# Cross-attention block on one core: reciprocals one slot later, sums behind copies and loads, a product stream spread over eight slots

## The chip, the cores and the metric

The kernel runs on one core of one Trainium2 chip. The metric is the device time of one execution in microseconds. Before the change three runs took 780.96, 783.5 and 778.15 us, a median of 780.96 us. The profile is of one further execution.

## The reference

Eight sequences of 256 tokens with 512 features attend to a context of the same shape, with 16 heads of 32 features, and an MLP of width 2048 follows. All is float32.

```
x   = layer_norm(hidden, ln1);  q = x @ q_w + q_b          # heads: 16 x 32
k   = enc @ k_w + k_b;          v = enc @ v_w + v_b
p   = softmax(where(mask, q @ k.T / sqrt(32), -max))
h   = (p @ v) @ cproj_w + cproj_b + hidden
y   = gelu(layer_norm(h, ln2) @ fc_w + fc_b) @ proj_w + proj_b
out = h + y
```

## The kernel before

The eight sequences are worked in four groups of two (512 tokens). A feature dimension lies on the partitions, in chunks of 128, for everything that is multiplied.

Every large product is a 2 by 2 block product with seven block multiplications instead of eight (`strassen`, L320 to L383): the pieces p0 to p6 each put four matmuls of 128x128 by 128x256 on PE (the trace shows two instructions for each) into one of two PSUM banks and empty the bank with ACT or DVE. Such a product needs sums of the quarters of both operands, made on DVE with `sum_up` (L164 to L167): s2, s3, s4 and a sum in place of 21 for the first operand (`A_SUMS`), t1, t2, t4 and a sum in place of 12 for the other (`B_SUMS`). xnT is the normalised and transposed x; kw, qw, vw, cw are the four weights of the attention; fcw and pw those of the MLP. Only the first product, k of group 0, is made with all eight terms (`eight`, L422), so that it needs no sums.

The attention runs over 32 units: unit n is a group, four heads (a quarter of the features) and one of the two sequences. For a unit, `scores` fills four PSUM banks, one for each head; `softmax(n, j)` takes the maximum of head j on DVE (L536) and the exponential on ACT (L546), which also gives the row sums; `divide` makes the reciprocals of the sums on DVE (L558) and scales the probabilities with four instructions on POOL (L560); `turn_probs` transposes head j on PE (L571) into one of two PSUM banks, emptied by DVE for head 0 (L574) and by ACT for the others (L576); `attend` multiplies with v (L587) and copies the result with the bias of v on DVE (L595).

The order on each engine is the order in which the code is written out; there is no scheduler. The loop near the end of the attention part has one slot for each unit. Slot n issues the scores and the softmax of unit n+2, and between them the transposes and the product of unit n. Into a slot of group g with number u (0 to 7) other work is hung by two tables: `between[g, u, 0..1]` holds the pieces of the block products of the next group and the transposes that feed them, `aside[g, u, 0..3]` holds loads, sums, layer norm parts (`norm_over`: statistics, then the inverse root on POOL at L193 and L194, then the normalisation on DVE at L197), bias additions on POOL (L483) and mask work. In the loop, `aside 0` stands ahead of the first transposes, `between 0` after head 1, `aside 1` after head 3, `between 1` after the last part of the softmax, `aside 2` ahead of `attend`, and `aside 3` at the slot's end. Below, slot n counts from 0 to 31; slot 8g+u belongs to (g, u).

Units 0 and 1 are prepared in a prologue, together with the projections of group 0. The projections of group g+1 are hung into group g; the last group has none to make, and takes the output projections (`project_out`, po) of groups 1 and 2 instead, and the first layer norm, transposes and weight sums of the MLP. The residual goes through POOL additions (L494) and is stored to DRAM by `store_hid`.

`cols` holds all bias and layer norm vectors as columns; they are loaded as 44 rows by the POOL queue, transposed on PE and copied by DVE.

The MLP runs over the four groups. In each, four steps q make two chunks of the hidden layer in both halves: seven block multiplications with fcw (L865, called pf), with DVE copies at L920, L922, L924, L932 and L937 and the GELU on ACT (L908), then differences on POOL (L940, L941). The second matrix follows (py). The sums of the quarters of proj_w, each 128x2048, are made in group 0 by `sum_pw` (L874), after the loads of pw have been issued by the SP queue.

Of the kernel before, what the change touches and what calls it, by code (L numbers as in the profile page):

```python
# [22 lines left out]
def tile_xattn_block(  # L23
# [45 lines left out]
    nc = tc.nc  # L69
# [37 lines left out]
    ident = const.tile([P, P], F32, name="ident")  # L107
# [6 lines left out]
    n_rows = sum(n for _, n in vecs)  # L114
    rows = const.tile([n_rows, P], F32, name="rows")
    cols = const.tile([P, n_rows], F32, name="cols")
# [47 lines left out]
    def sum_up(eng, x, table, *which):  # L164
        for i in which:
            to, a, b, op = table[i]
            eng.tensor_tensor(x[to], x[a], x[b], op)  # L167
# [75 lines left out]
    with ExitStack() as att:  # L243
# [23 lines left out]
        def turned(name):  # L267


            places[0] += 1  # L270
            if not pts and (places[0] % 2 or probs):
                return ps_t.tile([P, G], F32, tag="pt", name=name)
            return ps_s.tile([P, G], F32, tag="s", name=name)
# [148 lines left out]
        def eight(name, n, w, x, made):  # L422


            bank = ps_m.tile([P, 2, S], F32, tag=f"m{turns[0]}", name=f"{name}_{n}")
            turns[0] ^= 1
            for i in range(2):
                for c in range(NC):
                    nc.tensor.matmul(  # L429
                        bank[:, i, :],  # L430
                        w[f"{n[0]}{c // HC + 1}"][:, c % HC, ts(i, P)],
                        x[f"{c // HC + 1}{n[1]}"][:, c % HC, :],
                        start=i == 0 and c == 0,
                        stop=c == NC - 1,
                        skip_group_check=True,
                    )
            made(n, bank, None)

        def project_v(g):

# [114 lines left out]
        def divide(n):  # L555
            pr, (_, _, sums) = probs[n], stats.pop(n)
            rsum = small.tile([P, HPG, NQ], F32, tag="rsum", name=f"rsum_{n}")
            nc.vector.reciprocal(rsum, sums)  # L558
            for j in range(HPG):
                nc.gpsimd.tensor_tensor(  # L560
                    pr[:, j],
                    pr[:, j],
                    rsum[:, j, :, None].to_broadcast([P, NQ, SK]),
                    ALU.mult,
                )

        def turn_probs(n, j):
            ps = ps_t.tile([P, NK, S], F32, tag="pt", name=f"ppt_{n}_{j}")
            for kc in range(NK):
                for i in range(NQ):  # L570
                    nc.tensor.transpose(ps[:, kc, ts(i, P)], probs[n][:, j, i, ts(kc, P)], ident)  # L571
            pt = work.tile([P, NK, S], F32, tag="pt", bufs=4, name=f"pt_{n}_{j}")
            if j == 0:
                nc.vector.tensor_copy(pt, ps)  # L574
            else:
                nc.scalar.copy(pt, ps)  # L576
            pts[n, j] = pt
# [43 lines left out]
        def spread(g, places, pieces):  # L621

            for i, f in enumerate(pieces):
                begin(g, *places[min(i, len(places) - 1)], f)
# [32 lines left out]
        def sums_at(of_, g, places):  # L657
            spread(places[0][0], [p[1:] for p in places], [
                lambda i=i: sum_up(V, of_[g], B_SUMS, i) for i in range(4)
            ])  # L660
# [4 lines left out]
        ALL = (0, 1, 2, 3)  # L665
# [36 lines left out]
        for g in range(NG):  # L702
# [4 lines left out]
                    begin(g, 2 * hg, 2, sum_att, g, hg - 1)  # L707
            if g != 1 and g + 1 < NG:
                begin(g + 1, 0, 2, sum_att, g, NHG - 1)
        spread(0, [(0, 2), (3, 1), (5, 2), (5, 2)], [lambda i=i: sum_up(V, ws["c"], A_SUMS, i) for i in ALL])  # L710
        g = 1
        begin(g, 1, 3, load_res, 0)
        bias_at(0, g, [(2, 1), (2, 2), (3, 1), (3, 2)])
# [7 lines left out]
        share(  # L721
            g,
            project_out(1) + project_out(2),
            [(u, i, 1) for u in range(6) for i in range(2)] + [(6, 0, 1), (7, 0, 1)],
        )
        begin(g, 3, 3, load_res, 2)
        bias_at(2, g, [(4, 1), (4, 2), (5, 1), (5, 2)])
# [42 lines left out]
        load_ctx(1)  # L770
        ws["c"] = weight("cw", cproj_w)
        k, q, v, tx = project_qk(0, "kT"), project_qk(0, "qT"), project_v(0), turn_x(0)
        ps = turned("ps_cols")
        nc.tensor.transpose(ps[:, :n_rows], rows, ident[:n_rows, :n_rows])
        nc.vector.tensor_copy(cols, ps[:, :n_rows])
        seen, roots, normalise = layer_norm(xs[0], "a0")
        run([k[0], *seen, roots, k[1], *normalise])
        sum_up(V, ws["q"], A_SUMS, *ALL)
# [17 lines left out]
        for j, pieces in enumerate((v[1:2], v[2:3], tx[:2], v[3:4])):  # L796
            softmax(0, j)
            run(pieces)
        sum_up(V, ws["k"], A_SUMS, 2)
        divide(0)  # L800
        scores(1)
        for j, pieces in enumerate((v[4:5], tx[2:] + v[5:6], [], v[6:])):
            softmax(1, j)
            run(pieces)
        sum_up(V, xnT[1], B_SUMS, 0, 1)
        divide(1)
        sum_up(V, xnT[1], B_SUMS, 2, 3)
        sum_up(V, ws["k"], A_SUMS, 3)
        load_v(0, 0)
        load_qk(0, 2)  # L810

        for n, (g, hg, b) in enumerate(units):
            u = hg * GB + b
            ahead = n + 2 < len(units)
            if ahead:
                scores(n + 2)
                softmax(n + 2, 0)
            run(aside[g, u, 0])
            turn_probs(n, 0)
            turn_probs(n, 1)  # L820
            if ahead:
                softmax(n + 2, 1)
            run(between[g, u, 0])
            if ahead:
                softmax(n + 2, 2)
            turn_probs(n, 2)
            turn_probs(n, 3)
            run(aside[g, u, 1])
            if ahead:
                softmax(n + 2, 3)  # L830
            run(between[g, u, 1])
            run(aside[g, u, 2])
            attend(n)
            if ahead:
                divide(n + 2)
            run(later)
            later.clear()
            run(aside[g, u, 3])
# [10 lines left out]
    with ExitStack() as mlp:  # L849
# [21 lines left out]
        def sum_pw(i):  # L871

            to, a, b = (("t1", "12", "11"), ("t2", "22", "t1"), ("12", "22", "12"), ("t4", "21", "t2"))[i]
            nc.vector.tensor_tensor(pw[to], pw[a], pw[b], ALU.subtract)  # L874

        for g in range(NG):
# [21 lines left out]
            for q in range(HF // 2):  # L898
                bank = {
                    n: ps_f.tile([P, 2, S], F32, tag=f"f{n}", name=f"pf{n}_{g}_{q}") for n in (1, 6, 7, 5)  # L900
                }
                u1 = work.tile([P, 2, S], F32, tag="u1", bufs=1, name=f"u1_{g}_{q}")
                u2 = work.tile([P, 2, S], F32, tag="u2", bufs=2, name=f"u2_{g}_{q}")
                u3 = work.tile([P, 2, S], F32, tag="u3", bufs=1, name=f"u3_{g}_{q}")

                def gelu(n, half, src):
                    for i in range(2):
                        nc.scalar.activation(  # L908
                            h[n][q][:, i, :],
                            src[:, i, :],  # L910
                            AF.Gelu_apprx_tanh,
                            bias=col(c_fcb, half * HF + 2 * q + i),
                            scale=1.0,
                        )

                ahead = g == 0 and 1 < q + 2 < HF // 2
                fc(bank[1], "11", "11", q, True, False)
                nc.scalar.copy(u1, bank[1])  # L918
                fc(bank[6], "s2", "t2", q, True, True)
                nc.vector.tensor_tensor(u2, bank[6], u1, ALU.add)  # L920
                fc(bank[7], "s3", "12", q, True, False)
                nc.vector.tensor_tensor(u3, bank[7], u2, ALU.add)  # L922
                fc(bank[5], "21", "t1", q, True, False)
                nc.vector.tensor_tensor(h["22"][q], bank[5], u3, ALU.add)  # L924
                if ahead:
                    sum_fc(q + 2, 0, 1)
                fc(bank[1], "12", "21", q, False, True)

                gelu("11", 0, bank[1])
                gelu("22", 1, h["22"][q])  # L930
                fc(bank[7], "22", "t4", q, False, True)
                nc.vector.tensor_tensor(h["12"][q], bank[7], u2, ALU.add)  # L932
                if ahead:
                    sum_fc(q + 2, 2, 3)
                gelu("12", 1, h["12"][q])
                fc(bank[5], "s4", "22", q, False, True)
                nc.vector.tensor_tensor(h["21"][q], bank[5], u2, ALU.add)  # L937
                gelu("21", 0, h["21"][q])

                nc.gpsimd.tensor_tensor(h["s3"][q], h["11"][q], h["21"][q], ALU.subtract)  # L940
                nc.gpsimd.tensor_tensor(h["21"][q], h["21"][q], h["22"][q], ALU.add)  # L941
                if g == 0:
                    sum_pw(q)
                if q == 0:
                    ht = residual(work, hid_dram[g], "resm", f"resm_{g}")
                    nc.gpsimd.tensor_tensor(
                        ht, ht, projb[:, None, :].to_broadcast([P, NT, D]), ALU.add
                    )
                    if g + 1 < NG:
                        load_hid(g + 1)  # L950
# [114 lines left out]
```

## Time and profile before

| quantity | value |
|---|---|
| median of three runs | 780.96 us |
| lowest, highest run | 778.15 us, 783.5 us |
| profiled execution | 779.79 us, its span 778.0 us |
| granted PE clock, mean | 0.991 |
| busy: PE, PE weight load | 750.5 us, 628.1 us |
| busy: DVE, ACT, POOL | 414.1 us, 284.8 us, 309.4 us |
| prologue, to the first scores of the loop | 0 to 55.1 us |
| loop over 32 slots | 55.1 to about 365 us |
| last output projection and MLP | to 778.0 us |

A line of the timeline gives start, length, engine, source line, operation, output and inputs, the number of instructions merged, and in brackets the idle time before it with what ended that idle time. A line of the chain that ended last gives start, length, engine, tile and source line. The bars of matmuls overlap, so that PE's busy time is not a measure of its pace.

### The profile page before, as it was taken

The page shows a single profiled execution, that of the slowest core. Times are in us where ns is not written, and L with a number is a line of the kernel's source. Part 1 is how long each engine was busy: PE and PEld are TensorE (multiplying, and loading weights), DVE is VectorE, ACT ScalarE, POOL GpSimd, SP SyncE. Part 2 cuts the span into 40 slices and gives each one's busy share as a digit, 9 for nine tenths or more (in the row PEclk, how much of TensorE's full clock was granted, in tenths as well). Part 3 has the DMA queues.
Part 4 walks back from the last instruction along what each step waited for, and adds up shares of the span by engine and source line. Part 5 has one row for each costly group of instructions (what it writes and reads, how often), then busy time and mean ns, then how long its engine had stood idle before and what let it go on. Part 6 is the DMA issues. An engine that isn't in the chain of part 4 may idle for free.

```text
span 778.0 us, 12046 instructions
## 1 busy us (share of the span) xinstructions
PE 750.5 (96%) x4425; PEld 628.1 (81%) x4425; DVE 414.1 (53%) x1062; ACT 284.8 (37%) x833; POOL 309.4 (40%) x271
## 2 busy tenths in 40 slices
PE   6998999999999999988989999999999999999997
PEld 5887777777887767666878888888888888888886
DVE  4877787767576678796564651226412254222011
ACT  2265667755766667662232100421003220032200
POOL 3024344446544439784515550324503244032340
PEclk9998999999999999999999999999999999999999
DMA  9523422462225166521490002200012000110001
GB/s 300 204 69 114 148 95 70 140 204 82 82 96 167 56 203 216 168 78 61 147 333 3 0 1 75 88 1 1 1 58 105 1 0 1 55 56 0 1 1 54
DMA packets 55915, 68.70 MB, mean 88 GB/s; under 512 B 4740, under 2 KB 37552, under 8 KB 55728
## 3 DMA queue, kind: packets, MB, share of 16 engines
q1 hardware_dynamic: 55600, 67.91, 26.3%
q8 instruction: 35, 0.57, 0.3%
q14 instruction: 24, 0.20, 0.1%
q0 software_dynamic: 256, 0.02, 0.0%
HBM read 46.95 MB, written 20.97 MB: 87 GB/s over the span
## 4 chain that ended last, share of the span: by engine, by line
PE 76%; DVE 11%; ACT 4%; DMA 4%; POOL 3%; issue 2%; SPq 1%; DVEq 0%; POOLq 0%; ACTq 0%
PE py L865 25%; PE pf L865 22%; PE pv L337 4%; PE ppt L571 4%; PE pqT L337 4%; PE pkT L337 4%; PE po L337 3%; PE s L518 3%; ACT pr L546 3%; PE av L587 2%; PE pkT L429 2%; DVE pr L536 2%; DMA pw<-in_L_xattn_proj_w_dram 1%; POOL pr L560 1%; DVE fcw L167 1%
## 5 line engine op out<-in xcount | busy, mean ns | idle before, releaser
L865 PE MATMUL pf<-y,fcw 128*128 128x256 f32 x896 | 194.3, 379 | 2.8 <-DVE u L922 2.8
L865 PEld LDWEIGHTS pf<-y,fcw 128*128 128x128 f32 x896 | 170.2, 190 | 26.3 <-DVE u L922 3.2
L560 POOL TENSOR_TENSOR pr<-pr,rsum 128x512 f32<-128x512 f32 x128 | 131.2, 1056 | 130.0 <-DVE rsum L558 124.8
L546 ACT ACTIVATE pr<-pr,nmax 128x256 f32<-128x256 f32 x256 | 128.1, 503 | 98.7 <-DVE nmax L536 98.7
L536 DVE CUSTOM_DVE_ANT_0 pr<-s,mb 128x256 f32<-128x256 f32 x256 | 95.0, 414 | 7.1 <-PE s L518 6.5
L940 POOL TENSOR_TENSOR hs<-h,h 128x512 f32<-128x512 f32 x16 | 22.3, 1396 | 176.4 <-PE pf L865 127.5
L865 PE MATMUL py<-pw,h 128*128 128x256 f32 x384 | 84.8, 379 | 0.0
L865 PE MATMUL py<-pw_t,h 128*128 128x256 f32 x384 | 83.5, 379 | 0.0
L571 PE MATMUL ppt<-ident,pr 128*128 128x128 f32 x512 | 71.8, 280 | 11.8 <-DVE rsum L558 6.1
L571 PEld LDWEIGHTS ppt<-ident,pr 128*128 128x128 f32 x512 | 58.0, 142 | 28.6 <-issue 20.3
L865 PEld LDWEIGHTS py<-pw_t,h 128*128 128x128 f32 x384 | 72.7, 190 | 9.8
L865 PEld LDWEIGHTS py<-pw,h 128*128 128x128 f32 x384 | 72.7, 190 | 9.8
L918 ACT COPY u<-pf 128x512 f32<-128x512 f32 x16 | 9.4, 586 | 142.4 <-PE pf L865 141.0
L576 ACT COPY pt<-ppt 128x512 f32<-128x512 f32 x96 | 51.6, 571 | 12.6 <-PE ppt L571 12.6
L908 ACT ACTIVATE h<-h,cols 128x256 f32<-128x256 f32 x96 | 43.4, 501 | 28.9 <-DVE h L937 13.4
L337 PE MATMUL pv<-vw,ctxT 128*128 128x256 f32 x224 | 52.4, 380 | 0.0
L337 PE MATMUL pqT<-xnT,qw 128*128 128x256 f32 x224 | 52.2, 385 | 0.0
L908 ACT ACTIVATE h<-pf,cols 128x256 f32<-128x256 f32 x32 | 13.4, 471 | 99.8 <-PE pf L865 99.8
L546 ACT ACTIVATION_READ_ACCUMULATOR pr<-pr,nmax 128x1 f32 x256 | 48.5, 189 | 0.0
L337 PEld LDWEIGHTS pqT<-xnT,qw 128*128 128x128 f32 x224 | 42.4, 195 | 5.3
L337 PEld LDWEIGHTS pv<-vw,ctxT 128*128 128x128 f32 x224 | 41.0, 190 | 5.4 <-DVE x L197 0.3
L518 PE MATMUL s<-kT,qT 32*128 32x256 f32 x512 | 41.1, 403 | 0.5 <-DVE nmax L536 0.5
(118 smaller groups left out, 942.8 us busy)
## 6 DMA issues: line engine op xcount, KB each, us to landing
ctx<-in_ctx_dram SPq DMA_DIRECT2D x16, 256.0 KB, 4.3
x<-in_x_dram SPq DMA_DIRECT2D x16, 256.0 KB, 5.0
v_dram<-st_v SPq DMA_DIRECT2D x16, 256.0 KB, 2.1
v<-v_dram SPq DMA_DIRECT2D x16, 256.0 KB, 3.9
resx<-in_x_dram SPq DMA_DIRECT2D x4, 1024.0 KB, 6.6
hid_dram<-resx SPq DMA_DIRECT2D x8, 512.0 KB, 3.0
hm<-hid_dram SPq DMA_DIRECT2D x16, 256.0 KB, 5.7
fcw<-in_L_xattn_fc_w_dram SPq DMA_DIRECT2D x16, 256.0 KB, 6.0
```

The source lines that it names most:

```text
L337: nc.tensor.matmul(bank[n][:, i, :], l[:, c, ts(i, P)], r[:, c, :], start=first and i == 0 and c == 0, stop=last and c == HC - 1, skip_gro ...
L429: nc.tensor.matmul(bank[:, i, :], w[f"{n[0]}{c // HC + 1}"][:, c % HC, ts(i, P)], x[f"{c // HC + 1}{n[1]}"][:, c % HC, :], start=i == 0 an ...
L518: nc.tensor.matmul(banks[j][:, i, :], qT[j * HD : (j + 1) * HD, b * S + i * P : b * S + (i + 1) * P], kT[j * HD : (j + 1) * HD, b * SK : ( ...
L536: nc.vector.tensor_tensor_reduce(pr[:, j, i, :], banks[j][:, i, :], mbias[g][1][:, b, :], scale=-SCALE, scalar=FLT_MAX, op0=ALU.add, op1=A ...
L546: nc.scalar.activation(pr[:, j, i, :], pr[:, j, i, :], AF.Exp, bias=nmax[:, j, i : i + 1], scale=-1.0, accum_out=sums[:, j, i : i + 1],)
L560: nc.gpsimd.tensor_tensor(pr[:, j], pr[:, j], rsum[:, j, :, None].to_broadcast([P, NQ, SK]), ALU.mult,)
L571: nc.tensor.transpose(ps[:, kc, ts(i, P)], probs[n][:, j, i, ts(kc, P)], ident)
L576: nc.scalar.copy(pt, ps)
L587: nc.tensor.matmul(av[j * HD : (j + 1) * HD, :], vs[g, hg][:, b * NK + kc, ts(j, HD)], pts[n, j][:, kc, :], start=(kc == 0), stop=(kc == N ...
L865: nc.tensor.matmul(ps, lhsT, rhs, start=first, stop=last, skip_group_check=True)
L908: nc.scalar.activation(h[n][q][:, i, :], src[:, i, :], AF.Gelu_apprx_tanh, bias=col(c_fcb, half * HF + 2 * q + i), scale=1.0,)
L940: nc.gpsimd.tensor_tensor(h["s3"][q], h["11"][q], h["21"][q], ALU.subtract)
```

## The change

Five edits are made.

1. The transpose of the rows into `cols` and its copy move from ahead of the first product of k into `eight`, behind the matmuls of the quarter 11 and ahead of its evacuation.
2. Sums of xnT of group 1 and the sums 2 and 3 of kw leave the prologue. They are hung into slots 0 and 1 (xnT), and into slots 1 and 2 (kw), and the four sums of cw move from slots 0, 3 and 5 to slots 4 and 5.
3. `divide` is called for unit n+1 after the transposes of heads 0 and 1 in slot n, where it was called for unit n+2 at the end of slot n; unit 1 is thereby divided in slot 0 instead of the prologue.
4. The 14 pieces of the output projections of groups 1 and 2 in the last group are hung two into each of slots u = 0, 1, 2, 4, 5 and 6, and one into slots 3 and 7. Before, they were two in each of slots 0 to 5 and one in slots 6 and 7. The pieces of group 1 stay where they were.
5. The four sums of proj_w in the first group of the MLP: none in step 0, the first in step 1, the second and third in step 2, the fourth in step 3. Before, one in each step.

```diff
@@ eight
+            if n == "11":
+                turn_cols()
             made(n, bank, None)
+
+        def turn_cols():
+            ps = turned("ps_cols")
+            nc.tensor.transpose(ps[:, :n_rows], rows, ident[:n_rows, :n_rows])
+            nc.vector.tensor_copy(cols, ps[:, :n_rows])
@@ tables
-        spread(0, [(0, 2), (3, 1), (5, 2), (5, 2)], [lambda i=i: sum_up(V, ws["c"], A_SUMS, i) for i in ALL])
+        sums_at(xnT, 1, [(0, 0, 1), (0, 0, 1), (0, 0, 2), (0, 1, 1)])
+        spread(0, [(1, 2), (2, 2)], [lambda i=i: sum_up(V, ws["k"], A_SUMS, i) for i in (2, 3)])
+        spread(0, [(4, 2), (5, 1), (5, 2), (5, 2)], [lambda i=i: sum_up(V, ws["c"], A_SUMS, i) for i in ALL])
@@
             project_out(1) + project_out(2),
-            [(u, i, 1) for u in range(6) for i in range(2)] + [(6, 0, 1), (7, 0, 1)],
+            [(u, i, 1) for u in range(8) for i in range(2) if (u, i) not in ((3, 1), (7, 1))],
@@ prologue
         k, q, v, tx = project_qk(0, "kT"), project_qk(0, "qT"), project_v(0), turn_x(0)
-        ps = turned("ps_cols")
-        nc.tensor.transpose(ps[:, :n_rows], rows, ident[:n_rows, :n_rows])
-        nc.vector.tensor_copy(cols, ps[:, :n_rows])
...
-        sum_up(V, ws["k"], A_SUMS, 2)
         divide(0)
         scores(1)
...
-        sum_up(V, xnT[1], B_SUMS, 0, 1)
-        divide(1)
-        sum_up(V, xnT[1], B_SUMS, 2, 3)
-        sum_up(V, ws["k"], A_SUMS, 3)
         load_v(0, 0)
         load_qk(0, 2)
@@ loop
             turn_probs(n, 0)
             turn_probs(n, 1)
+            if n + 1 < len(units):
+                divide(n + 1)
             if ahead:
                 softmax(n + 2, 1)
...
             attend(n)
-            if ahead:
-                divide(n + 2)
             run(later)
@@ MLP
                 if g == 0:
-                    sum_pw(q)
+                    for i in ((), (0,), (1, 2), (3,))[q]:
+                        sum_pw(i)
```

## The prediction

> **What bounds the kernel now.** I read the page's busy shares first, then the chain that ended last, then the timeline where that chain leaves PE.
>
> ```profile
> PE 750.5 (96%) x4425; PEld 628.1 (81%) x4425; DVE 414.1 (53%) x1062; ACT 284.8 (37%) x833; POOL 309.4 (40%) x271
> ```
>
> PE looks full, but the matmul bars are longer than the pace of the stream: a 128x256 matmul is shown with 379 ns, while 16 of them take 3.46 us in the chain, 216 ns each. The chain is on PE for 76% only, so there is something to win, and only where PE stands still. The largest such place is the first slot of the loop over units:
>
> ```profile
> 56.88 0.69 DVE xnT L167
> 57.57 0.11 DVE rsum L558
> 57.68 2.00 DVE xnT L167 x2
> 59.69 1.44 DVE kw L167
> ...
> 61.82 0.61 DVE pt L574
> 62.43 0.14 issue
> 62.57 1.94 PE ppt L571 x8
> ```
>
> Five DVE sums (the first at 56.17, before these lines) stand ahead of the slot's softmax and copy (L574); the third transposed block (L571) needs the bank that this copy frees. PE then pays twice:
>
> ```profile
> 62.57 1.94 PE L571 MATMUL ppt<-ident,pr 128*128 128x128 f32 x8 [3.06 <-DVE pt L574]
> ...
> 55.10:71.70 16.60, 13.54 (x81) 10.86 (x80) 12.50 (x35) 9.09 (x31) 5.26 (x4) 0.79 0.24 80
> 71.70:81.80 10.10, 10.10 (x87) 8.18 (x83) 6.66 (x26) 6.34 (x21) 4.04 (x4) 1.00 0.51 163
> ```
>
> The last two rows are slots 0 and 1 (length, busy time of PE, PEld, DVE, ACT, POOL, granted clock, DMA). They hold the same PE instructions, yet slot 0 lasts 16.6 us and slot 1 10.1 us: 3.06 us of waiting, and a clock of 0.79 after it. The second large place is the first group of the MLP, where DVE sits on a load that nobody needs yet:
>
> ```profile
> 397.57 2.29 DVE L874 TENSOR_TENSOR pw_t<-pw,pw 128x2048 f32<-128x2048 f32 x1 [6.76 <-DMA pw<-in_L_xattn_proj_w_dram]
> ...
> 401.31 27.89 PE L865 MATMUL pf<-y,fcw 128*128 128x256 f32 x128 [2.80 <-DVE u L922]
> ```
>
> Third, the layer norm's root on POOL stands behind a 4 us scaling, and DVE waits for it:
>
> ```profile
> 102.52 4.03 POOL L560 TENSOR_TENSOR pr<-pr,rsum 128x512 f32<-128x512 f32 x4 [4.90 <-DVE rsum L558]
> ...
> 106.83 1.04 POOL L194 TENSOR_TENSOR rstd_a<-ve_a,neg_half 128x4 f32<-128x4 f32 x1
> ...
> 107.90 1.00 DVE L197 TENSOR_SCALAR x<-x,mv_a,rstd_a 128x512 f32<-128x512 f32 x2 [1.34 <-POOL rstd_a L194]
> ```
>
> **What the Trainium skill says.** "TensorE: Matmul & The Clock Gate", section Part 1: PE drops to half rate after an idle window of some 3.4 us. The trace agrees: the stretch 60 to 70 us has a granted clock of 0.66, which is 6.8 us at half rate, two such windows. "SBUF — State Buffer", section Who interferes with whom: a DVE instruction with two SBUF inputs contends with a GpSimd one that reads SBUF. The trace agrees: the kw sum (L167, 128x512) took 0.68 us at 48.52 and 1.52 us at 59.61, with POOL scaling beside it. "Perfetto Trace Analysis", section Identifying the Most-Contended Engine: matmul busy time is a poor measure of headroom, as seen above.
>
> **The change part by part.**
>
> *cols later.* The transpose and its copy move behind the eight-term product pkT_11. PE stood 1.12 us before it, so the first three of its four contraction steps can go ahead of the ACT copy that ends at 10.67; PE gains about 1.0. But the DVE copy of cols then waits for the end of that product, about 13.2 instead of 11.55. Behind it on DVE queue the statistics, the normalisation, the q sums, the xnT sums and the vw sums; DVE is without a gap but 1.49 (root) and 0.98 (pxt) until 30.3, when it frees the bank of the second q product. That bank was in time by 0.8 (free at 30.98, wanted at 31.75). DVE late by 1.6, less the 0.98 that it no longer waits, is ready near 31.5. So PE keeps 0.2; bounds +0.3 and -1.0.
>
> *Sums out of the prologue.* Four xnT sums and two kw sums leave DVE (at 0.69 uncontended, measured 5.1 for the last five with POOL beside them). Slot 0 then: scores to 56.3, softmax(2,0) to 57.0, copy to 57.9, so the third transposed block is not held. PE comes to the second q product at 57.61+1.73+0.87+0.87 = 61.1. It needs t2, which DVE now makes in this slot, after three softmax parts (59.4) and under POOL's scaling: two sums in 2.0 (the 57.68 row), so 61.4, with latency 61.55. From there slot 1 needed 81.77-77.22 = 4.55 to its end: slot 1 starts at 66.1 instead of 71.73. Gain 5.6, of which some 3.0 is the clock that no longer drops; bounds -4 and -6.5.
> What is late next: t4 and one kw sum now stand in slot 1, the other kw sum in slot 2. Both slots already end on DVE: the copy of the attention output (L595) comes 1.5 us after its matmuls in slot 1, and the second transposed block waits for it (0.27 and 0.19 at slots 2 and 3). t4 hides, since ACT is not ready for the next softmax part until 78.68; the kw sums stand directly ahead of L595: +0.7 +0.7 = +1.4 (0 to +2.8 if contended). Moving a cw sum out of slot 3 gives nothing back, since PE bounds there. In slot 5 a cw sum now precedes softmax(7,3), and through ACT the bank that the scores wait for: +0.5 (0 to +1.4).
>
> *Reciprocal and scaling later.* "One slot" is less in time: from the end of slot n to behind the first copy in slot n+1, in slot 3 from 93.22 to 94.6, 1.4 us. The scaling then ends at about 98.9, and PE wants it at 102.15: hidden by 3.2 us, and if that cover went, each late 128x512 costs 1.06. Nor is a wait of PE removed by taking the reciprocal from behind L595, although the profile names it as the releaser:
>
> ```profile
> 93.45 0.63 PE L571 MATMUL ppt<-ident,pr 128*128 128x128 f32 x4 [0.19 <-DVE rsum L558]
> ...
> 358.33 0.47 DVE L595 TENSOR_SCALAR att<-av,cols 128x256 f32<-128x256 f32 x1
> 358.95 1.08 PE L571 MATMUL ppt<-ident,pr 128*128 128x128 f32 x4 [2.55 <-DVE att L595]
> ```
>
> PE starts 0.62 after the start of L595 (92.83, 358.33) in both, and the second place has no reciprocal: L595 releases it. What does change is POOL's order: the roots now stand ahead of a scaling. DVE's 1.34 at 107.90 goes, and with it 0.4 of PE at slot 5 (four transposes from 111.31 are issued by 111.75 at 0.109 each; the next came at 112.17) and as much at slot 13, where the same happens: -0.8 (0 to -1.5). A bias addition that waits for its load (L483, at 291.56) moves ahead of scaling 24, which then runs 294.3 to 298.8; its first quarter is wanted at 297.97 and ready at 295.4: 0. The block also moves onto DVE sums in mid slot (134.72: two sums in 1.29, just after POOL ended); each may cost 0.7 there, mostly under PE: +0.3 (0 to +2).
>
> *Last group.* Here DVE bounds: PE waits 1.44, 1.73 and 2.55 for L595 at 341.83, 350.75 and 358.95. The earlier root takes 1.1 from DVE in slot 27. Shifting po_2's products takes a sum (0.6) and a wait for PE (0.5) from slot 29, but brings a second product and a sum to slot 30, where DVE waits for PE already (1.95): slot 30 grows from 8.2 to about 9.7. Sum -1.1 -0.1 -0.8 +1.5 = -0.5 (-3 if the half clock after 358.95, 0.82 over that slot, goes too; +1). The last product and the store behind it keep their place.
>
> *proj_w sums.* None in step 0, one in step 1, two in step 2. The load landed at 397.55, far ahead of the end of step 1 (405.9). PE's 2.80 goes in full. Two sums of 2.28 from 417.8 end at 422.4; the next DVE copies wanted 420.68 and 422.34, then end near 423.8, before the 424.06 of the following one. POOL, not the large sum, was stretched when they met (2.30 for 1.26 at 418.87). So -2.8 (-1.8 to -2.9).
>
> The sum: -0.2 -5.6 +1.4 +0.5 -0.8 +0.3 -0.5 -2.8 = -7.7. The profiled execution took 779.79 (span 778.0): 772.1. The three runs have a median of 780.96, 1.2 above it; 773.3 by that. I take 772.6.
>
> **The rivals.** *More comes free* (0.20): the last group's 2.55 shrinks below what drops the clock, and the kw sums hide: -7.7 -2 -1.4 = about 769. For it: 0.82 in that slot is 1.7 us of loss; against: slot 30 gets longer. *The sums move the stall* (0.22): contended at 1.4 each, slots 1, 2 and 5 pay +2.8 and +1.4 instead of +1.9, slot 0 gains 4: -7.7 +2.3 +1.6, about 776.5. For it: both slots end on DVE; against: POOL is idle when the kw sums come. *Slower* (0.03): scaling now overlaps DVE's two-input sums in every slot. 32 slots of +0.7 are 22 us; less 7.7, that is 794. It decides once more than 11 slots pay in full; against it stands that from 162 to 270 us PE hardly waits at all, so most slots have DVE slack. *A change that doesn't do what it says* is the reciprocal's part as a remover of waits, as shown; it is in the forecast.
>
> **How the numbers follow.** Forecast 0.55 (770.5 to 775), others as given. The range 769 to 777 takes in the bounds of slot 0, of the kw sums and of the last group. 1% is 7.8 us, about what a measurement of this kernel can tell from no change; it lies at 773.15, inside the forecast: faster 0.55 (0.35 of the forecast, and the first rival), same 0.42, slower 0.03.
>
> **What would show it.** Slot 0 of 11 us with a clock of 1.00; slots 1 and 2 each some 0.7 longer, with waits for L595; no wait of PE on L922 in step 1; roots ahead of the scalings, and DVE's wait at L197 gone; a second product in slot 30, and a wait near 2.5 in slot 31 still. The prediction falls if PE waits for L560, if the clock drops elsewhere, or if the statistics at the start are late enough to hold the q products by more than 1 us.

## The result and the profile after

The changed kernel takes 777.78 us (median of 20 runs, 774.98 to 781.52) against 780.76 us for the kernel before (20 runs, 776.09 to 785.32). The ratio is 0.996, 95% interval 0.9944 to 0.9977: a small gain, where the prediction had 772.6 us. The profiled execution of the changed kernel has a span of 775.9 us.

The page of the kernel after, busy times:

```profile
PE 749.7 (97%) x4425; PEld 627.7 (81%) x4425; DVE 419.7 (54%) x1062; ACT 285.5 (37%) x833; POOL 313.6 (40%) x271
```

The instruction counts are unchanged, yet DVE is 5.6 us busier (it was 414.1) and POOL 4.2 us busier. The same instructions have become longer. That is the first hint to what went wrong. (Lines have moved: the copy after `attend` is L602, the transposes L578, the copy of head 0 L581, the scaling L567, the reciprocals L565, the softmax maximum L543, the sums of the attention output L612, the MLP's matmuls L866. In the lines below, mb is the mask and hm the MLP's copy of the hidden rows.)

Slot 0 in the chain that ended last, the kernel after (start, length, engine, tile, line):

```profile
58.02 0.69 DVE pt L581
...
60.15 1.35 DVE xnT L167
61.49 0.02 issue
61.52 1.42 DVE xnT L167
62.94 0.04 issue
62.98 3.72 PE pqT L337 x16
...
79.19 0.68 DVE kw L167
79.87 0.41 DVE att L602
80.28 0.14 issue
80.41 0.63 PE ppt L578 x4
```

The copy that frees the bank (L581) now comes right after its transposes, as forecast, and the wait of 3.06 us is gone. The sums t1 and t2 of xnT, now inside the slot and under POOL's scaling, hold the second q product, and in slot 1 a kw sum stands ahead of L602. The timeline of PE and the windows of slots 0 and 1 (length; busy time of PE, PEld, DVE, ACT, POOL; granted clock; DMA share; GB/s) of the kernel after:

```profile
59.98 1.04 PE L578 MATMUL ppt<-ident,pr 128*128 128x128 f32 x8
...
62.98 3.29 PE L337 MATMUL pqT<-xnT,qw 128*128 128x256 f32 x14 [1.09 <-DVE xnT L167]
...
55.80:67.70 11.90, 10.81 (x85) 8.47 (x84) 10.49 (x32) 9.34 (x31) 4.93 (x4) 1.00 0.35 109
67.70:77.70 10.00, 10.00 (x84) 8.11 (x83) 7.80 (x27) 6.33 (x21) 4.48 (x4) 1.00 0.56 166
```

Slot 0 fell from 16.6 to 11.9 us, at a full clock. The MLP's first group, timeline of PE, kernel after:

```profile
399.78 27.36 PE L866 MATMUL pf<-y,fcw 128*128 128x256 f32 x126
426.98 1.24 PE L866 MATMUL py<-pw,h 128*128 128x256 f32 x5
```

There is no bracket in front of any pf matmul: the 2.80 us for the load of pw are gone.

So the two large gains came. What took them back shows when the traces are compared stage by stage. The stages are bounded by the start of the first scores, of the product with v in each slot (L594, L587 before), of the MLP and of its second matrix; the table has the differences to the kernel before. (us; slot n here runs from the product of slot n-1 to that of slot n; "slot 0" also holds the two units of the prologue; negative is shorter.)

| stage | after | scaling back (edit 3 undone) | edits 2 and 5 alone |
|---|---|---|---|
| start to first scores | +0.64 | -0.95 | +1.74 |
| slot 0 | -4.74 | -5.03 | -5.03 |
| slots 1 to 3 | +1.20 | +1.20 | +1.21 |
| slots 4 and 5 | +0.17 | +0.60 | +0.61 |
| slots 6 to 22 | **+1.96** | -0.03 | +0.01 |
| slots 23 to 31 | +1.78 | +1.41 | +0.89 |
| first matrix of MLP | -3.07 | -3.07 | -3.07 |
| whole span | -2.09 | -5.87 | -3.64 |

The stages between slot 0 and slot 22 repeat to a few hundredths in all kernels that share the edits concerned, with one exception: in the kernel with cols back, described below, PE's granted clock is halved for 3.41 us in slot 6 (a clock drop), which takes 1.6 us more there. The start and the last group do not repeat so well. The row to look at is the one from slot 6 to slot 22: of the three, only the kernel with edit 3 loses there. It loses at slot 6 (1.07), slot 8 (0.57) and slot 16 (0.29).

What delays slot 6, in the chain that ended last, kernel after:

```profile
113.26 0.89 DVE mb L262
114.15 1.44 DVE cw L167
115.59 0.33 DVE pr L543
...
117.06 0.67 ACT xnT L311
117.74 0.04 issue
117.78 1.79 PE s L525 x12
```

One cw sum of 128x512 adds 1.44 us to the chain there, and the mask's conversion (L262) 0.89; in the timeline they take 1.52 and 0.97. POOL scales beside them, as its timeline in the kernel after shows:

```profile
110.83 4.21 POOL L567 TENSOR_TENSOR pr<-pr,rsum 128x512 f32<-128x512 f32 x4 [5.54 <-DVE rsum L565]
```

Before, the block ran earlier in the slot, mostly beside softmax maxima and copies, which read PSUM and at most one tile of SBUF. These don't suffer: in the kernel after, the maximum (L543) takes 0.42 us and the copy of head 0 (L581) 0.68 to 0.69, under POOL and clear of it. In the kernel with the scaling back at the slot's end, the timelines of POOL and DVE give for the same two instructions:

```profile
108.08 4.04 POOL L567 TENSOR_TENSOR pr<-pr,rsum 128x512 f32<-128x512 f32 x4 [5.01 <-DVE rsum L565]
...
111.72 0.68 DVE L262 TENSOR_SCALAR mb<-mu 128x512 f32<-128x512 uint8 x1
112.32 0.68 DVE L167 TENSOR_TENSOR cw<-cw 128x512 f32<-128x512 f32 x1
```

POOL is done at 112.1, and both take 0.68. The Trainium skill, "SBUF — State Buffer", section Who interferes with whom, says that a DVE instruction with two SBUF inputs contends with a GpSimd instruction that reads SBUF; it gives no price. The traces do: of the twelve xnT sums in the loop, 2 overlapped POOL before (mean 1.09 us, the others 0.68), after the change 7 (mean 1.35). Of all DVE sums of the loop with two SBUF inputs, and the normalisations (L197), these overlap the scaling for at least a third of their time: 10 of 62 before, 19 of 63 after, 7 of 63 with the scaling back. L262 and L197 have one SBUF tensor; the same section lists their operation, `tensor_scalar`, among those that can contend in a mode with two ports. Whether they ran in such a mode no run shows, but they did contend: L197 took 0.54 clear of POOL and 1.13 (mean of three for x) under it.

### The profile page after: what moved, and what is told of

Its sections match the earlier page's. It is cut to its first block, busy times and chain, and to the rows that moved or that the text cites. A ratio compares the mean times of both kernels' runs of the same rounds, so it can differ in the third digit from the quotient of the medians.

```text
span 775.9 us, 12042 instructions
## 1 busy us (share of the span) xinstructions
PE 749.7 (97%) x4425; PEld 627.7 (81%) x4425; DVE 419.7 (54%) x1062; ACT 285.5 (37%) x833; POOL 313.6 (40%) x271
## 4 chain that ended last, share of the span: by engine, by line
PE 80%; DVE 10%; ACT 3%; DMA 3%; issue 2%; POOL 1%; SPq 0%; DVEq 0%; ACTq 0%; POOLq 0%
PE py L866 25%; PE pf L866 25%; PE po L337 6%; PE ppt L578 5%; PE pv L337 4%; PE pkT L337 4%; PE pqT L337 3%; PE s L525 3%; PE av L594 2%; ACT pr L553 2%; DVE pr L543 1%; DVE xnT L167 1%; ACT pt L583 1%; PE pyt L210 1%; DVE x L197 1%
## 5 line engine op out<-in xcount | busy, mean ns | idle before, releaser
L866 PE MATMUL pf<-y,fcw 128*128 128x256 f32 x896 | 194.0, 379 | 0.0
L866 PEld LDWEIGHTS pf<-y,fcw 128*128 128x128 f32 x896 | 170.2, 190 | 23.1
L567 POOL TENSOR_TENSOR pr<-pr,rsum 128x512 f32<-128x512 f32 x128 | 134.2, 1079 | 132.7 <-DVE rsum L565 82.3
L543 DVE CUSTOM_DVE_ANT_0 pr<-s,mb 128x256 f32<-128x256 f32 x256 | 94.2, 411 | 8.9 <-PE s L525 8.7
L866 PE MATMUL py<-pw,h 128*128 128x256 f32 x384 | 84.8, 379 | 0.0
L866 PE MATMUL py<-pw_t,h 128*128 128x256 f32 x384 | 83.5, 379 | 0.0
L578 PE MATMUL ppt<-ident,pr 128*128 128x128 f32 x512 | 71.6, 279 | 10.1 <-DVE att L602 9.8
L866 PEld LDWEIGHTS py<-pw,h 128*128 128x128 f32 x384 | 72.7, 190 | 9.8
L866 PEld LDWEIGHTS py<-pw_t,h 128*128 128x128 f32 x384 | 72.7, 190 | 9.8
L578 PEld LDWEIGHTS ppt<-ident,pr 128*128 128x128 f32 x512 | 57.7, 142 | 27.4 <-issue 23.5
```

The lines of the kernel that those rows point to most:

```text
L543: nc.vector.tensor_tensor_reduce(pr[:, j, i, :], banks[j][:, i, :], mbias[g][1][:, b, :], scale=-SCALE, scalar=FLT_MAX, op0=ALU.add, op1=A ...
L567: nc.gpsimd.tensor_tensor(pr[:, j], pr[:, j], rsum[:, j, :, None].to_broadcast([P, NQ, SK]), ALU.mult,)
L866: nc.tensor.matmul(ps, lhsT, rhs, start=first, stop=last, skip_group_check=True)
```

## The experiments

**Scaling back to the slot's end.** The kernel after without edit 3.

```diff
             run(pieces)
+        divide(1)
...
-            if n + 1 < len(units):
-                divide(n + 1)
...
             attend(n)
+            if ahead:
+                divide(n + 2)
```

> The changed kernel with one part undone: reciprocal and scaling of unit n+2 at the end of slot n again (unit 1 in the prologue). Theory (POOL's scaling, 1.4 us later, now runs beside DVE's two-input sums and normalisations in mid slot and stretches them to about double, which counts where DVE bounds): the fcw sum and the normalisation in slot 28 take 0.7 again instead of 1.5 and 1.2, attend of unit 29 comes at about 347 us instead of 349.3, slots 1 to 9 give back about 1 us less, time 775.5 to 776.5. Rival (the roots ahead of the scaling are worth more than the contention costs): DVE waits 1.1 to 1.3 us at L197 again in slots 4, 12 and 27, and the time is 0.5 to 1.5 us longer than the changed kernel, 778.3 to 779.3.

Measured: 774.09 us (6 runs, 772.55 to 775.55), ratio 0.9918 (0.9884 to 0.9952): the direction expected, and a larger gain. Edit 3 thus costs 3.7 us by the medians, 3.3 by the ratios. The interval overlaps that of the kernel after by a hair (0.9944 to 0.9952); three more kernels below with the scaling at the slot's end have upper bounds of 0.9940, 0.9942 and 0.9933, all clear of it. The traces put 2.0 of it in slots 6 to 22, as shown, and 0.3 in slot 0. Slots 4 and 5 go the other way by 0.43: there the earlier root is worth what was forecast. The rest lies in the last group, where PE's clock has a part in it (see below). DVE is busy for 412.9 us in this kernel, 6.8 less than in the kernel after, for the same instructions.

**Scaling later still.** The kernel after, with `divide(n + 1)` behind the transposes of heads 2 and 3 and the sums of `aside 1`.

```diff
             run(aside[g, u, 1])
+            if n + 1 < len(units):
+                divide(n + 1)
```

> The changed kernel with reciprocal and scaling of unit n+1 another half slot later, behind the sums of aside 1. Theory (what counts is which DVE instructions the 4 us of POOL lie beside): in mid slot the sums are clear of it again (xnT, fcw, cw in aside 1 at 0.7), but those of aside 2, directly ahead of L595, and the normalisation are now beside it and take 1.3 to 1.5; no gain over the changed kernel, 777 to 780. Rival (only mid slot is harmful, and any other place is as good as the slot's end): 774 to 775.5. Other rival (lateness itself: PE waits for the scaled probabilities): idle time of PE that L567 ends, several us in total.

Measured: 788.45 us (4 runs), ratio 1.0112 (1.008 to 1.0144). Waits of PE (total, times, longest), this kernel:

```profile
PE ppt L578 <- DVE att L602: 17.1, 13, 4.7
...
PE ppt L578 <- POOL pr L567: 3.6, 4, 2.1
```

and the same view of the kernel after, where no line names POOL:

```profile
PE ppt L578 <- DVE att L602: 9.8, 10, 2.7
```

That is well above the 777 to 780 expected. Both mechanisms act here. PE waits for late probabilities (3.6 us), and the scaling now lies on the sums that stand ahead of L602: 14 of the 24 sums of the attention output (L612, 128x256) take over 0.6 us, for 3 in the kernel after. The waits for L602 grow by 7.3 us. In the kernel after only the second is there: the cover of 3.2 us that the prediction gave the scaling did hold.

**No scaling.** The kernel after, where POOL multiplies one element of each row in place of the four tiles.

```diff
-            for j in range(HPG):
-                nc.gpsimd.tensor_tensor(
-                    pr[:, j],
-                    pr[:, j],
-                    rsum[:, j, :, None].to_broadcast([P, NQ, SK]),
-                    ALU.mult,
-                )
+            nc.gpsimd.tensor_tensor(
+                pr[:, 0, 0, 0:1], pr[:, 0, 0, 0:1], rsum[:, 0, 0:1], ALU.mult
+            )
```

> The changed kernel with the scaling left out: POOL multiplies one element of each row instead of the four 128x512 parts of a unit, so the probabilities stay unnormalised; all else is as in the changed kernel. Theory (contention of the scaling with DVE's sums is what the change loses): the sums of 128x512 take 0.7 wherever no other POOL work is near, slots 6, 8 and 27 to 29 are as short as with the scaling put back or shorter, 772.5 to 774.5. Rival (the loss is in the order on DVE or PE, not in contention): 777 or more.

Measured: 768.74 us (4 runs), ratio 0.9853 (0.9826 to 0.9881), 9.0 us under the kernel after and below the 772.5 to 774.5 expected. The instructions of the tile xnT on DVE (shortest, median, longest in ns), first this kernel:

```profile
L167 DVE TENSOR_TENSOR xnT<-xnT x16: 681/685/691, 26.4 to 218.4; 128x512 f32<-128x512 f32 x16
```

then the kernel after:

```profile
L167 DVE TENSOR_TENSOR xnT<-xnT x16: 674/689/1524, 25.6 to 222.2; 128x512 f32<-128x512 f32 x16
```

Without POOL's block no sum is longer than 0.69 us; with it the longest takes 1.52. Slot 0 is 1.35 us shorter than after: that is what t1 and t2 pay. Slots 6 to 22 stand at -0.23 against before, slots 23 to 31 at -1.61. So in its old place the scaling costs 0.2 in slots 6 to 22, in its new place 2.2. The reciprocals keep their new place on DVE in this kernel, so their place in DVE's order is not what those slots lose by. Lateness and contention are taken away alike; it is the lines above that name contention, together with DVE's busy time: 419.7 us after, 412.9 with the scaling back, 406.6 without scaling.

**Roots ahead by hand.** With the scaling back at the slot's end, the roots of the layer norm move from `aside 3` to `aside 2`, ahead of it: the useful half of edit 3.

```diff
-                    g, xs, g + 2, "a", [(2, 1), (2, 2), (3, 1), (3, 2), (3, 3), (4, 1), (4, 1), (4, 2), (4, 2)]
+                    g, xs, g + 2, "a", [(2, 1), (2, 2), (3, 1), (3, 2), (3, 2), (4, 1), (4, 1), (4, 2), (4, 2)]
...
-            g, hids, 0, "m", [(1, 1), (1, 2), (2, 1), (2, 2), (2, 3), (3, 1), (3, 2), (4, 1), (4, 2)]
+            g, hids, 0, "m", [(1, 1), (1, 2), (2, 1), (2, 2), (2, 2), (3, 1), (3, 2), (4, 1), (4, 2)]
```

> The changed kernel with the scaling at the slot's end again, and the layer norm's roots one step earlier, ahead of that scaling on POOL (behind the last statistics, in aside 2). Theory (both effects of the scaling's move can be had apart: no contention and no wait for the root): DVE's waits of 1.3 us at L197 in slots 4 and 27 go, 0.4 us is gained at slot 5 and at most 1 us in slots 27 to 29 against the kernel with only the scaling put back; 773 to 773.8. Rival (the waits at L197 are covered by PE): no difference from it, 774.1.

Measured: 773.73 us (6 runs, 771.47 to 776.96), ratio 0.9914 (0.9888 to 0.994). The trace shows -0.85 in slots 4 and 5 against the kernel without it (-0.25 for +0.60 in the table's terms); slots 6 to 22 stay at +0.01. The times can't tell 0.85 us from nothing with six runs each, so the gain rests on the trace.

**Edits 2 and 5 alone.** The kernel before with the moved xnT, kw, cw and proj_w sums.

```diff
-        spread(0, [(0, 2), (3, 1), (5, 2), (5, 2)], [lambda i=i: sum_up(V, ws["c"], A_SUMS, i) for i in ALL])
+        sums_at(xnT, 1, [(0, 0, 1), (0, 0, 1), (0, 0, 2), (0, 1, 1)])
+        spread(0, [(1, 2), (2, 2)], [lambda i=i: sum_up(V, ws["k"], A_SUMS, i) for i in (2, 3)])
+        spread(0, [(4, 2), (5, 1), (5, 2), (5, 2)], [lambda i=i: sum_up(V, ws["c"], A_SUMS, i) for i in ALL])
...
-        sum_up(V, ws["k"], A_SUMS, 2)
...
-        sum_up(V, xnT[1], B_SUMS, 0, 1)
...
-        sum_up(V, xnT[1], B_SUMS, 2, 3)
-        sum_up(V, ws["k"], A_SUMS, 3)
...
-                    sum_pw(q)
+                    for i in ((), (0,), (1, 2), (3,))[q]:
+                        sum_pw(i)
```

> The kernel before with two parts of the change alone: the sums moved out of the prologue (and those of cw with them) and the new places of the proj_w sums. cols, the scaling and the last group's products stay as they were. Theory (these two parts hold the whole gain, 4.7 less 1.2 in the first slots and 3.0 in the MLP): 774 to 775, as with the scaling put back. Rival (cols and the products are worth something of their own): above 776.

Measured: 775.9 us (6 runs), ratio 0.9938 (0.9914 to 0.9961): between the two expectations (774 to 775, and above 776), and better than the whole change by its median, though the intervals overlap. Its stages, in the table, are the cleanest evidence against edit 3: from slot 4 to slot 22 this kernel and the one with the scaling back agree within 0.05 us.

**proj_w alone.** The kernel before with edit 5.

```diff
-                    sum_pw(q)
+                    for i in ((), (0,), (1, 2), (3,))[q]:
+                        sum_pw(i)
```

> The kernel before with one part of the change alone: no sum of proj_w in step 0 of the MLP, one in step 1, two in step 2. Theory (PE's wait for L922 goes in full and nothing returns): the second matrix starts 2.8 us earlier against the start of the MLP, 777.9. Rival (two sums in step 2 hold PE): only 1 to 2 us, 779 to 780.

Measured: 778.27 us (20 runs), ratio 0.9965 (0.9949 to 0.9981), a gain of 2.7 us. In the trace the first matrix of the MLP's first group is 3.07 us shorter and every stage from slot 0 to slot 22 is unchanged within 0.1. The forecast of this part was right; in the trace the gain even lies a little beyond its bound of -2.9.

**cols back.** The kernel after without edit 1.

```diff
-            if n == "11":
-                turn_cols()
             made(n, bank, None)
...
         k, q, v, tx = project_qk(0, "kT"), project_qk(0, "qT"), project_v(0), turn_x(0)
+        turn_cols()
```

> The changed kernel with one part undone: the transpose and copy of cols stand ahead of the first k product again. Theory (the DVE copy of cols waits for that product, and everything behind it on DVE is late until the second q product's bank is freed late): the third q piece no longer waits for L358, the scores of unit 0 start at 40.5 us instead of 41.1, and the whole is 0.6 us faster than the changed kernel, 777.2. Rival (the 0.6 us is chance of the loads at the start, and PE's earlier k product is a gain): unit 0's scores stay at 41.1 or later, time 777.8 to 778.8.

Measured: 779.98 us (12 runs), ratio 0.9976 (0.9956 to 0.9996): 1.2 to 2.2 us worse than the kernel after, with overlapping intervals, and slower than either expectation. The trace doesn't support a gain of that size: the first scores come at 41.04, with the edit at 41.11. What the edit wins early, it pays at the second q product, whose bank DVE frees late. Timelines of DVE and PE, kernel after:

```profile
14.27 0.20 DVE L444 COPY cols<-ps_cols 128x44 f32<-128x44 f32 x1 [2.48 <-PE ps_cols L443]
...
32.28 1.99 PE L337 MATMUL pqT<-xnT,qw 128*128 128x256 f32 x8 [0.56 <-DVE pqT_u L358]
```

The prediction named this wait. The same edit undone in a second kernel, the one with the roots ahead:

> The kernel with the scaling at the slot's end and the roots ahead of it, with cols ahead of the first k product again. Theory (the new place of cols gives PE a start of 1 to 2 us on the first k product and takes 0.8 back at the second q bank, so it is worth 0.5 to 1.5 us): from the end of the first k quarter to unit 0's scores 26.1 us instead of 26.9, but the scores later on the whole, time 774.3 to 775.3. Rival (no net worth): 773.7 or less.

Measured: 773.67 us (6 runs), ratio 0.9909 (0.9876 to 0.9942), against 773.73 with the edit. Edit 1 has no net worth that can be seen; the 1.2 to 2.2 us in the first pair stay unexplained. PE's clock doesn't account for them: over all runs its mean is 0.9938 with cols back and 0.9942 in the kernel after.

**Products back.** The kernel after without edit 4.

```diff
-            [(u, i, 1) for u in range(8) for i in range(2) if (u, i) not in ((3, 1), (7, 1))],
+            [(u, i, 1) for u in range(6) for i in range(2)] + [(6, 0, 1), (7, 0, 1)],
```

> The changed kernel with one part undone: the pieces of the last group's output projections in the old slots. Theory (the spread itself costs, since it puts a second product and its DVE evacuation into slot 30, where DVE waits for PE and the attention's end hangs on DVE): slot 30 is about 1.3 us shorter and slot 29 about 0.7 longer than in the changed kernel, attention ends 0.5 to 1 us earlier, 776.8 to 777.3. Rival (the loss in the last group is the scaling's contention alone): slots 27 to 29 keep their stretched sums, and the end of the attention part moves by less than 0.3 us either way, 777.8.

Measured: 777.98 us (18 runs), ratio 0.9959 (0.9944 to 0.9973): no difference from the kernel after, as the rival had it. Against it slot 30 is 1.3 us shorter and slot 29 0.5 longer, as the spread implies. Slot 28 is 0.8 shorter, where a clock drop of the kernel after is missing, and slot 31 is 2.1 longer, with a clock drop that the kernel after lacks. And the same on the kernel with the roots ahead:

> The kernel with the scaling at the slot's end and the roots ahead of it, with the last group's output projection in its old slots. Theory (the spread only moves a product and its evacuations between slots 28 and 30): slot 30 about 1.3 us shorter, slots 28 and 29 together about as much longer, time within 0.7 us of 773.7. Rival (the spread is a gain once contention is gone): 774.5 or more.

Measured: 773.0 us (6 runs, 771.31 to 776.07), ratio 0.9901 (0.987 to 0.9933). This is the lowest median of all kernels that scale the probabilities, below both the kernel before and the changed one; it can't be told apart from its neighbours at 773.67, 773.73 and 774.09.

## Why the prediction was wrong

**Sums out of the prologue: right in mechanism, slot 0 too large by 0.9.** Slot 0 gained 4.74, inside its bounds, for 5.6. The mis-sized term is the pair t1 and t2: entered with 2.0 us from a pair that had POOL beside it for part of its time, it took 2.77 (1.35 and 1.42), and PE waited 1.09 for it. The kw sums cost 1.20 for 1.4, and the cw sum ahead of softmax(7,3) 0.60 for 0.5.

**Reciprocal and scaling later: the step that failed.** The prediction saw the block move onto DVE sums in mid slot, and entered "+0.3 (0 to +2)" on the ground that the rest lies under PE. With the root's gain of 0.8, and the 1.1 that it entered for the earlier root in the last group, it had -1.6 for edit 3. The runs give +3.3 to +3.7. The difference of some 5 us is about as large as the whole miss (-7.7 forecast, -3.0 by the medians). What it overlooked is who stands behind the stretched sum. A sum is stretched by 0.7 us, and in slot 6 the softmax behind it, the ACT copies behind that and the scores behind those pass it on to PE. The ground given for the "slower" rival's weakness, that PE hardly waits from 162 to 270 us, is right for that stretch (+0.29, at slot 16), but the loss sits outside it: 1.64 in slots 6 and 8, and, by the medians, nearly 2 in the last group. The rival "slower" named the right mechanism and was wrong in scale: not every slot pays, only those whose sums stand on a short path. The rival "the sums move the stall" came closest in number (776.5), but not by its own reckoning: it had slots 1, 2 and 5 pay 4.2 where they pay 1.8, and held nothing of edit 3's loss.

The last group, kernel after, timelines of POOL and DVE in slot 28 and of PE behind it:

```profile
333.28 4.67 POOL L567 TENSOR_TENSOR pr<-pr,rsum 128x512 f32<-128x512 f32 x4 [3.70 <-DVE rsum L565]
...
334.39 1.22 DVE L197 TENSOR_SCALAR hm<-hm,mv_m,rstd_m 128x512 f32<-128x512 f32 x1
...
335.53 1.52 DVE L167 TENSOR_TENSOR fcw<-fcw 128x512 f32<-128x512 f32 x1
...
342.27 0.99 PE L578 MATMUL ppt<-ident,pr 128*128 128x128 f32 x4 [2.47 <-DVE att L602]
```

The counterparts in the kernel before, timelines of DVE and PE:

```profile
335.80 0.67 DVE L197 TENSOR_SCALAR hm<-hm,mv_m,rstd_m 128x512 f32<-128x512 f32 x1
336.39 0.68 DVE L167 TENSOR_TENSOR fcw<-fcw 128x512 f32<-128x512 f32 x1
...
341.83 0.63 PE L571 MATMUL ppt<-ident,pr 128*128 128x128 f32 x4 [1.44 <-DVE rsum L558]
```

The normalisation and the sum have grown by 1.4 us together, and PE's wait from 1.44 to 2.47. This is the group that the prediction itself called bound by DVE; the contention should have been charged there in full.

The longer wait has a second price. The windows of slot 29 in the kernel after and in the one with the scaling back (granted clock 0.86 and 1.00, third number from the end):

```profile
337.00:349.28 12.28, 9.81 (x70) 7.71 (x69) 10.27 (x30) 6.62 (x24) 9.23 (x8) 0.86 0.08 23
```

```profile
332.92:343.50 10.58, 8.53 (x70) 6.35 (x69) 9.96 (x29) 6.42 (x22) 7.89 (x7) 1.00 0.04 11
```

The 1.70 us between them are about what one clock drop costs, and the kernel after has one right behind the wait of 2.47. The traces of the three kernels with the scaling in edit 3's place (after, cols back, products back) all have a drop there, with waits of 2.33 to 2.48; the other nine have none there, with waits of at most 2.06. By the mean granted clock of all runs, the kernel after is short of 4.5 us of full clock (20 runs, 0.9942) and the one with the scaling back of 2.4 (6 runs, 0.9968). So an estimate from these means gives about 2 of the 3.7 us of edit 3 to the clock. One sign by which the prediction said it would fall, a clock drop elsewhere, did come; PE's waits for the scaling, and a hold of the q products of over 1 us at the start, did not.

The rest of that step held. The root for slot 5 is done ahead of the scaling, and DVE's wait at L197 is gone. Timelines of POOL and DVE, kernel after:

```profile
99.37 1.04 POOL L194 TENSOR_TENSOR rstd_a<-ve_a,neg_half 128x4 f32<-128x4 f32 x1
101.08 4.22 POOL L567 TENSOR_TENSOR pr<-pr,rsum 128x512 f32<-128x512 f32 x4 [0.67 <-DVE rsum L565]
...
103.58 1.99 DVE L197 TENSOR_SCALAR x<-x,mv_a,rstd_a 128x512 f32<-128x512 f32 x2
```

It brought 0.43. The other 0.4, at slot 13, didn't come: in the kernel before the root ends there at 187.17 and DVE reaches L197 at 187.34, without an idle moment. The prediction had carried the wait over from slot 5 unread. (In the last line the two normalisations take 1.99 us together, for 1.00 before: here too POOL is beside them.) And the point that the reciprocal releases nobody was right: with it moved away, the same waits of PE carry the name of L602.

**Last group.** Forecast -0.5 (-3 to +1); in the profiled execution slots 23 to 31 cost +1.78. With edit 4 undone the time is the same, so the size isn't the spread's; edit 3 adds 2.4 us in slots 27 to 29 in one pair of traces, the 1.7 of the clock drop included. The wait in slot 31 stayed, 2.71 for 2.55, as foretold.

**cols** was entered with -0.2 and is worth nothing that shows. **proj_w** was entered with -2.8 and measured -3.07 in the trace, -2.7 in the times.

Without edit 3 the forecast's own terms give -7.7 + 0.8 - 0.3 + 1.1 = -6.1, or 774.7 us against the median of 780.76. That kernel measured 774.09. The stages of its trace account for -5.87; the start, which differs from execution to execution, and the last group make the rest uncertain by 1 to 2 us.

## What to carry to other kernels

Before moving a POOL block in time, list the DVE instructions that it will newly lie beside, with their inputs: a 128x512 sum of two SBUF tiles costs 0.7 us more under it, while softmax maxima and copies out of PSUM kept their length. Then follow each stretched instruction to the next one that PE waits for; a share of busy time, or "PE hardly waits here", doesn't do that for the slots where DVE stands on the path. An edit that makes one small instruction earlier, like the roots here, is better made by moving that instruction than the block in front of it.

## What the runs showed of the hardware

The clock drops of PE are of a fixed length. In the record of the granted clock each lasts 3.41 us, at half the clock. The kernel before shows them at 61.6 to 68.4 (two) and at 358.5; the kernel after at 328.7 and 342.4; the kernel with the roots ahead has none before its last matmul, though PE waits 2.61 us in slot 31 there, as it does where the clock drops. (A drop behind the last matmul, in every trace, costs nothing.) The Trainium skill, "TensorE: Matmul & The Clock Gate", section Part 1, says that the activity window is free-running and that its effect differs between runs of one kernel; these traces agree. It ties the drop to an idle window of some 3.4 us, as the prediction repeats. There the measurement differs: PE had stood still for 3.06 and 2.55 us ahead of the drops of the kernel before, for 1.91 and 2.47 ahead of those of the kernel after. Keeping the waits under 3.4 us is thus not enough here. One drop costs up to 1.7 us (half of 3.41); the one in slot 6 of the kernel with cols back took 1.6. The drops also make much of the spread between runs: of the 20 runs of the kernel after, the ten fastest have a mean clock of 0.994 to 1.000, the ten slowest of 0.992 to 0.994, and 0.008 of 776 us are 6.2 us, for 6.5 between the fastest and the slowest. It is not all: the runs at 0.992 alone lie from 777.84 to 781.52. A single trace is thus a poor judge of the last group.

A load in mid loop adds to it. DVE waits for the first `att_in` tile in every trace, with all later DVE work behind it. The shortest of those waits is in the kernel before, the longest in the kernel with roots ahead and products back (timelines of DVE, in this order):

```profile
286.23 0.69 DVE L167 TENSOR_TENSOR att_in<-att_in 128x512 f32<-128x512 f32 x1 [1.98 <-DMA att_in<-att_dram]
```

```profile
284.56 0.69 DVE L167 TENSOR_TENSOR att_in<-att_in 128x512 f32<-128x512 f32 x1 [3.86 <-DMA att_in<-att_dram]
```

From the first of the four issues to this sum it is 5.4 us in the one and 7.3 in the other; the second execution lost 3.3 us in that slot against the kernel with the scaling back, a clock drop included. Whether an earlier issue of these loads would win that time was not tried.
